# Graph attention and four residual layers on one core: own places for every job of the attention loop, and a reordered last phase

## The chip, the cores and the metric

The kernel runs on one core of one Trainium2 chip. Five engines work side by side, each with its own instruction queue worked off in order: PE (TensorE, matmuls and transposes), DVE (VectorE), ACT (ScalarE), POOL (GpSimd) and SP (SyncE, here only DMA issues). An instruction that needs another engine's result waits on a semaphore, and everything behind it in its queue waits too. The metric is the device time of one execution in microseconds (us); less is better.

## The reference

Sixteen graphs (B = 16) of N = 1024 nodes with F = 128 features and a weighted, symmetric-pattern adjacency of about 9 neighbours a node go through four layers, each `x = layernorm(x + layer(x))`:

```python
# layer 0: graph attention
pre = (h_self @ A1_i)[:, :, None, :] + (h_nb @ A1_j)[:, None, :, :] + A1_b
scores = where(adjacency == 0, -1e9, (relu(pre) @ A2_w)[..., 0] + A2_b[0])
out = relu(h_self + einsum('bij,bjf->bif', softmax(scores), h_nb))
# layer 1: a row-by-row dilation of the pattern, three SAGE convolutions with batch norm, then
out = concatenate([h1, h2, h3], -1) @ Wl + bl
# layer 2
out = relu(adj @ (x @ W + b) + x)
# layer 3
A1 = A + eye(N);  d = rsqrt(sum(A1, -1))
out = ((A1 * d[:, :, None] * d[:, None, :]) @ x) @ B
```

## The kernel before, in words

Four phases follow one another: attention (`phase_att`), the dilation pattern, the convolutions, and End (`phase_end`, which does the sum over the three convolutions, layer 2 and layer 3).

**Attention.** A graph's 1024 nodes are cut into ten groups of 104 (the last has 88). A *block* is one row band of group pairs, `band(r)`: 11 *units*, each a pair (i, j) of groups. Five blocks (r = 0 to 4) make a batch of 55 units; 16 batches make 80 blocks. The neighbours inside a unit are put into up to 128 slots. For each unit PE gathers the projected rows of both ends by one-hot matrices (`gather`, L506, lines 516 and 521), DVE scores both directions (`score`, L533), ACT takes the exponential and weighs the rows (`weigh`, L543 and L545), and three units later PE scatters them into the PSUM sums (`scatter`, L554) with a one-hot matrix that DVE makes (`numbered`, L501). A unit with i = j has one direction ("one way"), the others two.

The one-hot matrices of a block come from a chain of *jobs* that run one to three blocks ahead: counts and offsets of the slots; `beyond` (L369, POOL: the step table g, 1 where the slot number plus one exceeds the unit's offset, else 0, in pieces of 4, 4 and 3 units); `ranks` (L380, PE); `steps` (L409, PE, from g), `others` (L424, PE), `one_way` (DVE), `widen` (ACT), `numbers`. Each batch also makes the ten *projections* of the next one (`projection`, L297: two matmuls into a bank, then six readers of the bank: high, other_z and own on ACT, low, add_z and the self score on DVE, lines 315 to 321), its mask rows (L280 and L282 on POOL, with a load before and a store behind on SP), and the end of the one before: collects of the sums (`collect`, DVE, L565), clears of the sums (`clear`, PE, L264), ten `end_group` on DVE (L598 to L601 and statistics), `end_root` on POOL, ten `end_norm` on ACT (L619), stores, and three `end_turn` (transposes into a bank, read by ACT at L639).

All of these jobs that need PE products put them into a pool of two PSUM banks (`ps_w`, name pw). A new job takes the bank that comes free, and its first matmul waits until the last reader of the previous content is done. The main loop runs over units; for unit u of a block it issues in order: what is due (`later`), the block's jobs for that u, the gather, the products of the job, `numbered`, the score, *all* readers of the job one after the other, the weighing, a scatter. u = 0 to 2 holds the three steps, 3 to 5 the others, 6 and 7 a projection each, 8 to 10 ranks with counts, offsets and numbers. `as_traced` (L131) fixes each engine's order to that of the program from `first` on, in attention only.

**End.** For each batch b: eight tiles of `layer2` (`neighbours` is eight matmuls into one PSUM tile, L1647; DVE L1661 to L1664 and statistics; after tiles 3 and 7 `root`, whose power is on POOL at L1587, and d at L1668 or L1673; after tile 5 `apply` of half 0, DVE L1591), `turn` of both halves (PE transposes L1619, read by ACT L1620), `values_3`, eight tiles of `layer3`. Woven in is the first step of batch b+1: `bias_1` (POOL, L1575), `products_1` (PE, L1603) and `rows_1` (DVE: the sum at L1608, then four tiles' statistics and the root), `apply`, `turn`, `values_2`. `store_slots` (L1519) writes rows kept from the pattern phase into the x rows of batch b+4: two indirect DMAs on POOL, issued in layer 2's tile 5. Their order on the engines is left to the scheduler here.

Of the kernel before, what the change touches and what calls it, by code (L numbers as in the profile page):

```python
# [23 lines left out]
P = 128  # L24
# [86 lines left out]
def constants(arrays):  # L111
# [13 lines left out]
    arrays["k_next"] = np.ascontiguousarray(np.broadcast_to(i + 1, (P, P)).astype(np.float16))  # L125
# [5 lines left out]
def as_traced(tc, first):  # L131

    last = {}
    for i in tc.nc.cur_bb.bb.instructions[first:]:
        if i.engine in last:
            tc.add_manual_dep(
                i, last[i.engine].name,
                mybir.DependencyInfo(mybir.DependencyClass.NoSync, mybir.DependencyReason.DATA),
                reason="as_traced",
            )  # L140
        last[i.engine] = i


@with_exitstack
def phase_att(ctx, tc, t, c, x1_d, x1T_d, mask_d, flags):
# [27 lines left out]
    k_next = load("k_next", [P, C])  # L173
# [123 lines left out]
    def projection(b, s):  # L297

        d = S[b]

        def products():
            pw = d.pw = ps_w.tile([P, 512], F32, name="pw")
# [8 lines left out]
        def readers():  # L311
            pw = d.pw
            hi = d.parts[s] = lp.tile([P, 2, 3 * F], F32R, name=f"parts{s}", bufs=1 if s < 4 else 2)
            z = sm.tile([P, F], F32, name="z_self", bufs=2)
            nc.scalar.copy(hi[:W, 0, :], pw[:W, : 3 * F])
            nc.scalar.copy(z[:W], pw[:W, 2 * F : 3 * F])
            nc.scalar.copy(d.own[:W, s, :, :F], pw[:W].rearrange("p (a f) -> p a f", f=F)[:, ::3, :])  # L317
            nc.vector.tensor_tensor(hi[:W, 1, :], pw[:W, : 3 * F], hi[:W, 0, :], ALU.subtract)  # L318
            nc.vector.tensor_tensor(z[:W], pw[:W, F : 2 * F], z[:W], ALU.add)
            k = b * NG + s  # L320
            nc.vector.scalar_tensor_tensor(
                z[:W], z[:W], 0.0, w_a2[:W], op0=ALU.max, op1=ALU.mult, accum_out=seen_self[:W, k : k + 1]
            )

        return products, readers
# [43 lines left out]
    def beyond(v, n0, m):  # L369

        if n0 == 0:
            v.g = sm.tile([P, UNITS, C], F16, name="g", bufs=1)
        g = v.g[:E, n0 : n0 + m, :]
        nc.gpsimd.tensor_tensor(  # L374
            g, k_next[:E].unsqueeze(1).to_broadcast([E, m, C]),
            v.off[:, n0 : n0 + m].unsqueeze(2).to_broadcast([E, m, C]), ALU.subtract,
        )
        nc.gpsimd.tensor_scalar(g, g, 1.0, 0.0, op0=ALU.min, op1=ALU.max)  # L378
# [77 lines left out]
    def bank_job(*parts):  # L456

        bank = []

        def products():  # L460
            bank.append(ps_w.tile([P, 512], F32, name="pw"))
            for f, g, args, at in parts:
                f(*args, bank[0][:, at:])

        def readers():
            for f, g, args, at in parts:
                g(*args, bank[0][:, at:])

        return products, readers

    def block_job(x, s):

        if s < 6:
            v = block(x + 1)
            f, g = ((steps, copy_steps), (others, copy_others))[s // 3]
            return [bank_job((f, g, (v, *pieces()[s % 3]), 0))] if v else []
        v, w, z = block(x + 2), block(x + 3), block(x + 1)
        parts = []
        if v:
            parts.append((ranks, copy_ranks, (v, *pieces()[s - 8]), 0))  # L480
        if s == 8 and w:
            parts.append((counts, copy_counts, (w,), 4 * W))
        if s == 10 and w:
            parts.append((offsets, copy_offsets, (w,), 4 * W))
        if s == 10 and z:
            parts.append((numbers, copy_numbers, (z,), 4 * W + 16))
        return [bank_job(*parts)] if parts else []
# [170 lines left out]
    def run(*parts):  # L658
        for f in bank_job(*parts):
            f()  # L660

    for x in range(3):
        v = block(x)
        run((counts, copy_counts, (v,), 0))
        run((offsets, copy_offsets, (v,), 0))
        if x == 2:
            break
        for n0, m in pieces():
            beyond(v, n0, m)
        for n0, m in pieces():  # L670
            run((ranks, copy_ranks, (v, n0, m), 0))
        if x == 1:
            continue
        for f, g in ((steps, copy_steps), (others, copy_others)):
            for n0, m in pieces():
                run((f, g, (v, n0, m), 0))
                if f is others:
                    widen(v, n0, m)
        run((numbers, copy_numbers, (v,), 0))
        for half in range(2):  # L680
            one_way(v, half)
    first = len(nc.cur_bb.bb.instructions)
    ORDER = (*range(4, NG), *range(4))
    SLOTS = BANDS * UNITS
    END_GROUP = (6, 7, 10, 11, 16, 17, 21, 22, 27, 28)
    owed, later = [], {}
    ld = {}

    def do(at, f, *args):
        later.setdefault(at, []).append((f, args))  # L690

    def mask_step(b, s):
        store = mask_rows(b, s, ld.pop((b, s)))
        do(at + 3, store)

    for b in range(1, B):
        base = (b - 2) * SLOTS + 40
        for s in range(NG):
            when = base + 4 * s if b > 1 else 3 * s
            do(max(when - 3, 0), lambda b, s: ld.update({(b, s): load_mask_rows(b, s)}), b, s)  # L700
            do(when, mask_step, b, s)
    for at in range(B * SLOTS):
        b, n = divmod(at, SLOTS)
        r, u = divmod(n, UNITS)
        x = at // UNITS
        for f, args in later.pop(at, []):
            f(*args)
        jobs = []
        if u in (6, 7):
            if b + 1 < B:  # L710
                jobs.append(projection(b + 1, ORDER[2 * r + u - 6]))
        else:
            jobs += block_job(x, u)
        v = block(x + 1)
        if v and u in (2, 4):
            one_way(v, u == 4)
        if v and 3 <= u < 6:
            do(at + 1, widen, v, *pieces()[u - 3])
        v = block(x + 2)
        if v and u in (4, 6, 8):  # L720
            beyond(v, *pieces()[u // 2 - 2])
        if b + 1 < B:
            if n == 5:
                begin(b + 1)
            if n == 53:
                do(at + 1, self_weight, b + 1)
        if b:
            if n == 0:
                end_load(b - 1)
            if 3 <= n < 6:  # L730
                collect(b - 1, n - 3)
            if n == 4:
                end_seen(b - 1)
            if n == 6:
                end_divide(b - 1)
                nc.gpsimd.memset(OWN[(b - 1) % 2][:W, :, 0, F : F + 1], 1.0)
            if n in END_GROUP:
                end_group(b - 1, ORDER[END_GROUP.index(n)])
            if n == 30:
                end_root(b - 1)  # L740
            if 33 <= n < 33 + NG:
                end_norm(b - 1, n - 33)
            if n == 45:
                end_store(b - 1)
            if n in (46, 48, 50):
# [1712 lines left out]
```

## Time and profile before

| | us |
|---|---|
| three runs | 3035.19, 3040.84, 3047.08 (median 3040.84) |
| the profiled execution | 3058.9 |
| its span, from first to last instruction | 3056.8 |
| mean granted PE clock | 0.937 |
| attention, about 62 to 1520 | 1458 |
| pattern, about 1520 to 2000 | 480 |
| convolutions, about 2000 to 2335 | 335 |
| End, about 2335 to 3056 | 721 |

The page begins with each engine's busy time and share of the span, and the span in 40 slices, where a digit is the busy share in tenths:

```profile
PE 2723.7 (89%) x25724; PEld 2392.3 (78%) x25724; DVE 2191.9 (72%) x8416; ACT 1860.8 (61%) x5689; POOL 1426.8 (47%) x1545
...
PE   5999999999999999999968888578796999999997
...
DVE  5788888888888888888863567756664666666664
ACT  3888888888888888888862233255654233343332
POOL 3766665666666666666313331244333333233321
PEclk8999999999999999999987777789997999999999
```

A row of a group of instructions has: line, engine, operation, output and input tiles with their shapes, count, then total busy time and mean ns of one, then the engine's idle time ahead of them and who ended it. The groups that the change touches on POOL and DVE:

```profile
L280 POOL TENSOR_SCALAR mask<-ld 104x1024 f16<-104x1024 f32 (+1 forms) x150 | 426.5, 2843 | 39.6 <-DMA ld<-in_adjT 39.4
L374 POOL TENSOR_TENSOR g<-k_next,off 105x512 f16<-105x512 f16 (+1 forms) x240 | 236.4, 985 | 366.4 <-PE pw L411 360.9
L378 POOL TENSOR_SCALAR g<-g 105x512 f16<-105x512 f16 (+1 forms) x240 | 188.7, 786 | 20.7
L318 DVE TENSOR_TENSOR parts<-pw,parts 104x384 fp32r<-104x384 f32 x160 | 88.9, 556 | 123.2 <-ACT own L317 122.0
L1591 DVE TENSOR_SCALAR x<-x,mv,rstd 128x128 f32<-128x128 f32 x256 | 104.7, 450 | 91.2 <-POOL rstd L1587 91.2
```

A row of waits has the engine and line that waited, the instruction it waited for, then total us, how often, and the longest. A timeline row has start, duration, engine, line, operation, tiles and count, and in brackets the idle time ahead of it and what ended it. Instructions of one line in a row are put together (x4). On PE a record's end is modelled and records overlap, so the spacing of starts is the better measure of cost there.

### The profile page before, as it was taken

Reading aid. Unit: us, or ns where it says so; the run is one execution under the profiler, and the core shown is the slowest. Engines: PE = TensorE matmul, PEld = TensorE weight load, DVE = VectorE, ACT = ScalarE, POOL = GpSimd, SP = SyncE. Lnnn points to the kernel's source line nnn. Section 1 sums busy time; section 2 is a strip of 40 time slices with the busy share of each in tenths; the row PEclk is TensorE's granted clock in tenths of the full one; section 3 lists DMA queues with packets and bytes.
Section 4 is the critical chain, followed back from the end, with each engine's and each line's share of the span. In section 5 each row is a group of like instructions: output and inputs, shape, how many; then the busy total and the mean of one; then the engine's idle time right before and its main releaser. Section 6 shows DMA issues by size and latency. Waiting matters only on the chain.

```text
span 3056.8 us, 70983 instructions
## 1 busy us (share of the span) xinstructions
PE 2723.7 (89%) x25724; PEld 2392.3 (78%) x25724; DVE 2191.9 (72%) x8416; ACT 1860.8 (61%) x5689; POOL 1426.8 (47%) x1545
## 2 busy tenths in 40 slices
PE   5999999999999999999968888578796999999997
PEld 3877777777777777777768887377786999999997
DVE  5788888888888888888863567756664666666664
ACT  3888888888888888888862233255654233343332
POOL 3766665666666666666313331244333333233321
PEclk8999999999999999999987777789997999999999
DMA  5323332233322333223026442054455354445440
GB/s 145 100 73 96 102 95 81 71 99 98 93 79 75 103 98 93 76 73 97 22 58 210 145 150 60 17 178 160 169 193 192 113 181 161 147 146 181 160 152 16
DMA packets 179958, 348.60 MB, mean 114 GB/s; under 512 B 14148, under 2 KB 89942, under 8 KB 179472
## 3 DMA queue, kind: packets, MB, share of 16 engines
q1 hardware_dynamic: 173584, 328.15, 33.7%
q0 software_dynamic: 4864, 11.63, 1.3%
q10 hardware_dynamic: 1152, 4.19, 0.5%
q8 instruction: 206, 3.38, 0.5%
q14 instruction: 152, 1.25, 0.1%
HBM read 257.87 MB, written 87.03 MB: 113 GB/s over the span
## 4 chain that ended last, share of the span: by engine, by line
PE 46%; DVE 28%; ACT 9%; issue 7%; DMA 6%; POOL 3%; SPq 0%; POOLq 0%; ACTq 0%; DVEq 0%
PE pg L1647 10%; PE pa L554 5%; DVE junk L533 5%; PE pg L516 4%; PE pg L521 3%; PE pq L1357 3%; DVE we L501 2%; DMA x_d<-keep_xs,keep_row 2%; ACT hg L545 2%; DVE oh_b L435 2%; DVE one_way L403 2%; PE pg L1007 2%; ACT oh L441 2%; DVE st L78 2%; DVE x_rows L601 2%
## 5 line engine op out<-in xcount | busy, mean ns | idle before, releaser
L545 ACT ACTIVATE hg<-pg,hg 128x128 f32<-128x128 f32 x1600 | 510.2, 365 | 28.6
L554 PE MATMUL pa<-hg,we 128*104 128x129 f32 (+1 forms) x3520 | 526.1, 272 | 0.0
L516 PE MATMUL pg<-parts,oh 104*128 104x384 f32 (+1 forms) x1760 | 512.8, 373 | 3.5 <-ACT hg L545 3.3
L554 PEld LDWEIGHTS pa<-hg,we 128*104 128x104 f32 x3520 | 447.7, 171 | 46.5 <-issue 38.2
L533 DVE SCALAR_TENSOR_TENSOR junk<-pg,w_a 128x128 bf16<-128x128 f32 x1600 | 396.7, 281 | 110.9 <-PE pg L521 104.4
L280 POOL TENSOR_SCALAR mask<-ld 104x1024 f16<-104x1024 f32 (+1 forms) x150 | 426.5, 2843 | 39.6 <-DMA ld<-in_adjT 39.4
L521 PE MATMUL pg<-parts,oh 104*128 104x384 f32 (+1 forms) x1760 | 434.3, 328 | 0.0
L374 POOL TENSOR_TENSOR g<-k_next,off 105x512 f16<-105x512 f16 (+1 forms) x240 | 236.4, 985 | 366.4 <-PE pw L411 360.9
L521 PEld LDWEIGHTS pg<-parts,oh 104*128 104x128 f32 x1760 | 311.4, 189 | 0.0
L543 ACT ACTIVATE hg<-sc 128x2 f32<-128x2 f32 (+1 forms) x880 | 187.8, 213 | 160.8 <-DVE junk L533 147.4
L516 PEld LDWEIGHTS pg<-parts,oh 104*128 104x128 f32 x1760 | 268.8, 191 | 21.5 <-ACT oh L441 15.1
L501 DVE TENSOR_TENSOR we<-k_id,ids 128x832 f32<-128x832 f16 (+1 forms) x240 | 259.2, 1080 | 9.3 <-PE pa L554 8.7
L1587 POOL TENSOR_TENSOR rstd<-ve,mhalf 128x4 f32<-128x4 f32 x96 | 97.0, 1011 | 323.9 <-DVE ve L1586 323.8
L441 ACT CAST oh<-oh_b 104x1024 fp32r<-104x1024 bf16 (+1 forms) x240 | 233.4, 973 | 1.0 <-DVE oh_b L435 1.0
L378 POOL TENSOR_SCALAR g<-g 105x512 f16<-105x512 f16 (+1 forms) x240 | 188.7, 786 | 20.7
L303 PE MATMUL pw<-w_all,xT 128*104 128x512 f32 x320 | 172.1, 620 | 24.7 <-ACT x1T L639 9.4
L318 DVE TENSOR_TENSOR parts<-pw,parts 104x384 fp32r<-104x384 f32 x160 | 88.9, 556 | 123.2 <-ACT own L317 122.0
L1591 DVE TENSOR_SCALAR x<-x,mv,rstd 128x128 f32<-128x128 f32 x256 | 104.7, 450 | 91.2 <-POOL rstd L1587 91.2
L435 DVE TENSOR_TENSOR oh_b<-pw,k_slot_edge 104x512 bf16<-104x512 f32 (+1 forms) x240 | 152.6, 636 | 5.6 <-PE pw L427 5.6
L1696 ACT ACTIVATE y<-x,shift,rstd 128x128 f32<-128x128 f32 x128 | 52.7, 482 | 162.9 <-POOL shift L1689 162.9
L403 DVE SCALAR_TENSOR_TENSOR one_way<-qs,mask 104x1040 bf16<-104x1040 f16 (+9 forms) x160 | 146.7, 917 | 1.1 <-ACT qs L396 1.1
L420 ACT CAST oh_b<-pw 104x512 bf16<-104x512 f32 (+1 forms) x240 | 131.2, 547 | 20.4 <-PE pw L411 20.0
(349 smaller groups left out, 6522.1 us busy)
## 6 DMA issues: line engine op xcount, KB each, us to landing
ld<-in_adjT SPq DMA_DIRECT2D x135, 416.0 KB
m<-mask_d SPq DMA_DIRECT2D x16, 2048.0 KB
keep_adj<-in_adjT SPq DMA_DIRECT2D x8, 4096.0 KB
adj<-in_adjT SPq DMA_DIRECT2D x8, 4096.0 KB
mask_d<-mask SPq DMA_DIRECT2D x144, 208.0 KB
hT_d<-uT SPq DMA_DIRECT2D x48, 512.0 KB
h<-hT_d SPq DMA_DIRECT2D x48, 512.0 KB
hT<-hT_d SPq DMA_DIRECT2D x32, 512.0 KB
```

Of the source, the lines that this page charges most:

```text
L280: engine.tensor_scalar(mt[:n, s, :N], ld[:n], 0.0, None, op0=ALU.is_gt)
L374: nc.gpsimd.tensor_tensor(g, k_next[:E].unsqueeze(1).to_broadcast([E, m, C]), v.off[:, n0 : n0 + m].unsqueeze(2).to_broadcast([E, m, C]), ...
L403: nc.vector.scalar_tensor_tensor(junk[:W, :nb, :], v.q[:W, at : at + nb, :W], EDGE, v.mt[:W, i, i * W : NP].rearrange("p (n w) -> p n w", ...
L435: nc.vector.tensor_tensor(v.o[:W, n0 : n0 + m, 1, :], pw[:W, : m * C].rearrange("p (n c) -> p n c", c=C), k_slot_edge[:W].unsqueeze(1).to_ ...
L441: nc.scalar.copy(v.ends[:W, n0 : n0 + m], v.o[:W, n0 : n0 + m])
L501: nc.vector.tensor_tensor(we[:, :n, :], k_id.unsqueeze(1).to_broadcast([P, n, W]), V[b * BANDS + r].ids[:, 2 * lo : 2 * hi].unsqueeze(2).t ...
L516: nc.tensor.matmul(flat[:, first : 3 * F], own, d.parts[i][:W, p, first:], start=p == 0, stop=False, skip_group_check=True,)
L521: nc.tensor.matmul(pg[:, 1::step, :], other, reversed_parts(d.parts[j][:W, p, :], step), start=False, stop=p == 1, skip_group_check=True,)
L533: nc.vector.scalar_tensor_tensor(junk, pg[:, 1 + e, :], 0.0, w_a2, op0=ALU.max, op1=ALU.mult, accum_out=d.sc[:, at + e : at + e + 1],)
L545: nc.scalar.activation(hg[:, e, :F], pg[:, 3 - 3 * e, :], AF.Copy, scale=hg[:, e, F : F + 1])
L554: nc.tensor.matmul(PA[bank][:W, at : at + part.stop - part.start], we[:, 2 * (u - lo) + e, :], hg[:, e, part], start=False, stop=True, ski ...
L1647: nc.tensor.matmul(pg[:, :cols], ADJ[b % 2][:, jt, it * P : (it + 1) * P], v[:, jt, :cols], start=jt == 0, stop=jt == T - 1,)
```

## The change

In attention every job's products and every single reader get a key: a place in units from the start of the block, with a fraction that orders it among the gather (.2), score (.49), weighing (.7) and scatter (.8) of that unit. All entries of all blocks are sorted by their key and issued in that order. A key may lie in the next block (over 11) or the one before (below 0). AHEAD says for which block the job is done. Jobs of the prologue are now the same entries, from block -3 on. The six readers of a projection are taken in the order high, other_z, own, low, add_z, self, at the keys of PROJECT behind the first, in ascending order of the keys.

```diff
+BANKS = (
+    (-1.1, (("step", 0),)), (0.38, (("step", 1),)), (0.72, (("step", 2),)), (1.82, (("other", 0),)),
+    (2.82, (("other", 1),)), (4.52, (("rank", 1),)), (5.3, (("rank", 0), ("count", 0),)), (5.42, (("other", 2),)),
+    (6.38, (("rank", 2), ("number", 0), ("offset", 0),)),
+)
+READ = {
+    ("step", 0): -0.9, ("step", 1): 0.48, ("step", 2): 1.65, ("rank", 0): 5.54, ("count", 0): 5.52, ("other", 0): 1.9,
+    ("other", 1): 3.95, ("other", 2): 5.75, ("rank", 1): 4.58, ("rank", 2): 8.31, ("offset", 0): 6.75,
+    ("number", 0): 8.95,
+}
+PROJECT = (
+    (6.3, 6.95, 6.42, 7.15, 7.25, 6.72, 10.58), (9.85, 10.02, 10.38, 11.1, 10.52, 11.32, 15.02),
+)
+BEYOND = (3.42, 3.48, 6.32)
+NUMBERED = (0.51, 6.9, 9.3)
+ONE_WAY = (-1.48, 0.52)
+WIDEN = (2.25, 6.33, 7.25)
+SCORE, WEIGH, SCATTER = 0.49, 0.7, 0.8
+COLLECT = (2.9, 5.56, 4.54)
+CLEAR = (4.72, 6.3, 5.78)
+DIVIDE = 6.45
+END_GROUP = (6.53, 9.52, 14.34, 8.02, 21.05, 28.95, 24.48, 26.53, 16.25, 28.34)
+END_ROOT = 30.1
+END_NORM = (37.34, 39.56, 36.15, 33.54, 41.3, 33.65, 33.82, 43.52, 44.56, 40.6)
+END_STORE = 45.1
+TURN = ((47.1, 47.48), (48.34, 48.51), (51.56, 52.56))
+MASKS = (-92.64, -89.49, -72.95, -66.46, -62.48, -54.95, -50.1, -47.1, -43.44, -37.5)
+AHEAD = {"step": 1, "other": 1, "number": 1, "rank": 2, "count": 3, "offset": 3}
...
+    for x in range(-3, B * BANDS):
+        b, r = divmod(x, BANDS)
+        at = x * UNITS
+        for u in range(UNITS if x >= 0 else 0):
+            do(at + u, 0.2, open_gather, b, r, u)
+            do(at + u, SCORE, take, score, b, r, u)
+            do(at + u, WEIGH, take, weigh, b, r, u)
+            do(at + u, SCATTER, scatters, b, r * UNITS + u)
...
+    for key, _, f, args in sorted(todo, key=lambda t: t[:2]):
...
+        f(*args)
     as_traced(tc, first)
```

The step table becomes one comparison for each unit, against a table now held in f32:

```diff
-        nc.gpsimd.tensor_tensor(
-            g, k_next[:E].unsqueeze(1).to_broadcast([E, m, C]),
-            v.off[:, n0 : n0 + m].unsqueeze(2).to_broadcast([E, m, C]), ALU.subtract,
-        )
-        nc.gpsimd.tensor_scalar(g, g, 1.0, 0.0, op0=ALU.min, op1=ALU.max)
+        for n in range(n0, n0 + m):
+            nc.gpsimd.tensor_scalar(v.g[:E, n, :], k_next[:E], v.off[:, n : n + 1], None, op0=ALU.is_gt)
```

In End `rows_1` is split into `add_1` (the sum) and `stats_1` (statistics and root), `apply(b, 0)` comes behind bias_1, `store_slots` issues one of its two DMAs behind layer 3's tile 3 and the other behind tile 5, the matmul loops of `turn` and `neighbours` run backwards, and `as_traced` holds the order of the whole phase:

```diff
             if more and it == 4:
                 bias_1(b + 1)
-            if it == 5 and b + 4 < B:
-                with tc.issue_after(S[b].first.ins):
-                    store_slots(nc, x1_d, keep, b + 4)
+            if it == 5:
+                apply(S[b], 0)
         turn(b, 0)
         if more:
             products_1(b + 1, 0, range(4))
-            rows_1(b + 1, 0)
-        values_3(b, 0)
+            add_1(b + 1, 0)
         apply(S[b], 1)
         if more:
             products_1(b + 1, 1, range(2))
         turn(b, 1)
+        for half in range(2):
+            values_3(b, half)
         if more:
             products_1(b + 1, 1, range(2, 4))
-        values_3(b, 1)
+            stats_1(b + 1, 0)
+            add_1(b + 1, 1)
         for it in range(T):
             layer3(b, it)
             if more:
                 if it == 0:
-                    rows_1(b + 1, 1)
                     apply(S[b + 1], 0)
+                if it == 1:
+                    stats_1(b + 1, 1)
                 if it == 2:
-                    apply(S[b + 1], 1)
                     turn(b + 1, 0)
                 if it == 3:
-                    turn(b + 1, 1)
+                    apply(S[b + 1], 1)
...
                 if it == 5:
-                    values_2(b + 1, 1)
+                    turn(b + 1, 1)
                     store(b, 0)
+                if it == 6:
+                    values_2(b + 1, 1)
                 negative(b + 1, it)
+            if it in (3, 5) and b + 4 < B:
+                store_slots(nc, x1_d, keep, b + 4, (it - 3) // 2)
```

## The prediction

> **What bounds the kernel now.** I read the windows by stage first, then what TensorE (PE) waits for in each, then the order of events round these waits. By stage:
>
> ```profile
> core 0: us, PE busy (x) PEld busy (x) DVE busy (x) ACT busy (x) POOL busy (x), PEclk, DMA share, GB/s
> 62.00:1520.00 1458.00, 1390.01 (x12050) 1151.26 (x12049) 1212.03 (x5229) 1225.57 (x3927) 923.36 (x874) 1.00 0.31 86
> 1520.00:2000.00 480.00, 362.54 (x5742) 325.11 (x5741) 293.40 (x962) 158.16 (x431) 142.19 (x218) 0.75 0.34 108
> 2000.00:2335.00 335.00, 277.99 (x2154) 250.70 (x2154) 210.74 (x304) 196.94 (x712) 134.89 (x190) 0.92 0.49 174
> 2335.00:3056.00 721.00, 665.74 (x5634) 651.45 (x5634) 446.46 (x1829) 261.38 (x572) 207.89 (x234) 0.95 0.41 143
> ```
>
> The rows are attention, dilation pattern, convolution layers and End. The change rewrites the first and the last. In attention PE is busy 1390 of 1458 us at full clock, DVE 83%, ACT 84%: PE's matmuls are the same after the change, so waits can give 68 us there at most, and two engines with little slack can take it back. In the stretch 100 to 1500 us this is all that PE waits for:
>
> ```profile
> PE pw L383 <- DVE z_self L319: 33.9, 43, 1.0
> PE pa L264 <- DVE own L565: 12.6, 14, 1.3
> PE pw L303 <- ACT x1T L639: 9.4, 14, 0.7
> PE pw L427 <- DVE oh_b L435: 3.8, 13, 0.3
> PE pw L303 <- DVE oh_b L435: 3.3, 14, 0.2
> ```
>
> 63 us over 13 to 14 batches: ranks waiting for a projection's reader, the clear for a collect, and bank reuse. Over steady batches (period 95.9 us) I count 4.63 us of PE idle each, 15 such batches. One instance, PE then DVE:
>
> ```profile
> 779.94 0.40 PE L521 MATMUL pg<-parts,oh 104*128 104x256 f32 x2
> 781.06 0.34 PE L383 MATMUL pw<-cnt,k_offs 104*128 104x416 f16 x1 [0.72 <-DVE z_self L319]
> ```
>
> ```profile
> 779.39 0.29 DVE L533 SCALAR_TENSOR_TENSOR junk<-pg,w_a 128x128 bf16<-128x128 f32 x1
> 780.16 0.56 DVE L318 TENSOR_TENSOR parts<-pw,parts 104x384 fp32r<-104x384 f32 x1 [0.48 <-ACT own L317]
> 780.64 0.28 DVE L319 TENSOR_TENSOR z_self<-pw,z_self 104x128 f32<-104x128 f32 x1
> ```
>
> The bank may be overwritten only after L319 at 780.92; PE starts .14 us later. That is what a bank wait looks like: last reader's end plus .15.
>
> In End PE's one large wait is the second turn (L1619): 22.3 us in 11 waits between 2400 and 2900. POOL shows why, then PE and DVE:
>
> ```profile
> 2587.93 1.14 POOL L1521 DMA_INDIRECT x_d<-keep_xs,keep_row  x1 [0.19 <-issue]
> 2594.11 0.97 POOL L1521 DMA_INDIRECT x_d<-keep_xs,keep_row  x1 [5.04 <-DMA x_d<-keep_xs,keep_row]
> 2595.09 1.05 POOL L1673 TENSOR_TENSOR d<-deg,mhalf 128x4 f32<-128x4 f32 x1
> 2596.11 1.00 POOL L1587 TENSOR_TENSOR rstd<-ve,mhalf 128x4 f32<-128x4 f32 x1
> 2597.09 2.33 POOL L1575 TENSOR_TENSOR x<-x,keep_bl 128x1024 f32<-128x1024 f32 x1
> ```
>
> ```profile
> 2596.21 1.50 PE L1603 MATMUL pp<-keep_wl,h 128*128 128x128 f32 x12
> 2599.57 1.10 PE L1619 MATMUL pt<-ident,x 128*128 128x128 f32 x4 [1.86 <-DVE x L1591]
> 2600.51 2.72 PE L1603 MATMUL pp<-keep_wl,h 128*128 128x128 f32 x12
> ```
>
> ```profile
> 2597.15 3.14 DVE L1591 TENSOR_SCALAR x<-x,mv,rstd 128x128 f32<-128x128 f32 x4 [3.38 <-POOL rstd L1587]
> ```
>
> The second store waits in POOL's queue for the first; the statistics' power L1587 waits behind it; apply L1591 waits for that; PE stands still 1.86 us. After it the same twelve products take 2.72 us instead of 1.50 and the turn 1.10 instead of .60.
>
> **The change in End.** Turn to turn, batches 1 to 11 take 43.76 us on average, batches 12 to 14 (no store_slots) 40.26. Removing the store from this place is worth the difference, 3.50 us, and its parts agree: idle 2.03 (22.3/11) plus 1.72 of slow matmuls in 9 of the 11 = 3.43. 11 x 3.50 = 38.5 us. The two stores go behind layer 3's tiles 3 and 5. POOL then stands up to 6 us there, and behind it are only root and shift of tile 7, wanted by a store that comes in the next layer 2: nothing, unless the second pair is later than that half.
>
> Added: add_1 of the next batch now stands in DVE's queue ahead of apply(b,1), which turn(b,1) needs. From the end of layer 2 (T): turn .44 + products half 0 2.67 = 3.11; +.2 until DVE starts; add_1 .67 (L1608); four applies at .28 (1.11 for four with POOL idle); +.15: turn(b,1) can start at T+5.2. PE, with values_3(b,0) moved behind the turn, is there at T+3.11+1.33 = 4.44. A wait of .65 to .75, and .15 to .2 at layer 3's start, where ACT still scales v: .85 us in 14 batches = 11.9. End: -38.5 + 11.9 = **-27**. Ends: -38 if the wait is hidden; if each wait is followed by half-speed matmuls, +1.72 more in 14 batches: -3. I take no slowdown, since attention's idles of .7 to 1.07 us show none behind them. The Trainium skill, "TensorE: Matmul & The Clock Gate", Part 1, lets the clock fall only after an idle window of some 3.4 us; the 1.86 us here were enough, so the row decides; by the rule the slow matmuls have another cause and might stay, which would make End -27 + 9 x 1.72 = -11.5.
>
> The reversed turn and neighbours loops let PE wait once, for the last value: the same sum. Earlier h loads (SP) cost no engine.
>
> **The change in attention.** Same matmuls, same DVE and ACT operations; only their places differ, and POOL's beyond, which is two passes of 512 or 384 elements (mean 985 and 786 ns in the page's groups; 3 pieces, 5.3 us a block) and becomes 11 comparisons of 128. Bounds for one: .3 us (slope of L378 between its shapes) and .52 (L280's 2.5 ns an element plus .2): 3.3 to 5.7 us a block. POOL is busy 63% here and the tables are read several units later: nothing, either way.
>
> Now the waits. Most of those listed go: each clear stands .7 to 1.8 units behind its collect, and the ranks no longer meet a fresh projection's bank. Mask rows (L280, 2.84 us of POOL each) come earlier, and their loads and stores with them in SP's queue, ahead of which nothing is late. But new waits come. The two banks are handed out as they come free, and the third step product (key .72) takes the bank of the second projection (9.85). So it waits for add_z (key 11.32, in front of score 0). From the end of unit 10's gather, DVE: .2 latency, two scores .42, self .22, low .47, add_z .28, .15 to PE = 1.74 us. PE meanwhile has scatter .36, a one-way gather .55, step product 1 .23 = 1.14. A wait of **.6 us in every block**, 3.0 a batch: this is L383's wait at another line. In the fifth block the second turn (key 48.34) takes a bank of the first projection: .8. So 3.8 a batch where DVE and ACT otherwise keep up. They don't everywhere: the first block holds three end groups (1.25 us of DVE each) and a collect, and walking DVE there gives 2.45 us of waits, the fourth has six of the norms, 1.63 with ACT nearly full, the others .78, .94, 1.5: 7.3 a batch. The same walk made on the kernel before falls short of its row by some .3 a block, so it isn't generous. Behind these step products wait the next gather and, through it, score and weigh of the new block. I take the middle, 5.5, against 4.63: 15 x .87 = **+13**. Ends: 3.0 (-24) and 7.3 (+40).
>
> A new prologue does the same work interleaved: 0, within 3 us. Pattern and convolution keep their order: 0.
>
> Sum on the profiled execution: 3056.8 - 27 + 13 = 3042.8 span. It ran 3058.9, 0.6% over the median 3040.84; the same -14 from the median gives **3027**.
>
> **A rule that speaks against it.** apply L1591 x4 takes 1.11 us with POOL idle and 3.14 beside bias_1 (L1575). In the new order bias_1 follows layer 2's tile 3 on POOL and may meet apply(b,0) behind tile 5, ahead of turn(b,0). The Trainium skill, "SBUF — State Buffer", section "SBUF: two separate sides", says why: the port pair that DVE and GpSimd share is held for a whole instruction and the other blocks, as the 3.14 shows. By rule and row the price is the one in rival D.
>
> **Rivals.**
> A, the above: own range 3005 to 3045.
> B, the waits in attention shrink to the .6 of each block because DVE's and ACT's loaded spots lie where PE has work: 15 x (3.0 - 4.63) = -24, with End -27: 2990. For it: DVE idles 110 us before its scores, waiting for PE. Against: the walk on the old kernel gave too little.
> C, slower: DVE and ACT fall behind in the first, fourth and fifth blocks, so that projections' banks come free late: +40, prologue +3, End -27: 3041 + 16 = 3057. It decides from 6.4 us of waits a batch, where attention eats End's gain (4.63 + 27/15). For it: 83% and 84% busy, and the longer chain in front of the third step product.
> D, the store's wait is replaced in End: bias_1 holds apply(b,0) up by 2.03 us (3.14 - 1.11). DVE is through tile 5 some 1 us plus the four applies before turn(b,0), so PE waits about 1.05 us, 14 times = 15, and 24 more if matmuls run slow behind it: End -12 to +12, with +13: 3042 to 3066, I say 3050. Against: bias_1 should end before tile 5 does, as it starts when d's power ends and tiles are 1.81 us apart.
>
> **How the numbers follow.** A .38, B .22, C .30, D .10. The measurement can tell about 0.5%, 15.2 us, from no change: bounds 3025.6 and 3056.0. Faster: half of A, all of B = .41. Within: .17 of A, .06 of D, .08 of C = .31. Slower: .22 of C, .04 of D, .02 of A = .28. Range: 2985 (B with End at -32) to 3064 (C with its waits a little longer).
>
> **What would show it.** Right: no PE wait at the ranks' line for z_self, but .5 to .9 us at the step line on add_z in most blocks; End's turn(b,1) idle .5 to .9 instead of 2; End's period 41 us; POOL's store pair behind layer 3. Wrong: End's twelve products still at 2.7 us, or PE idle over 1 us at turn(b,0) (D); a batch of attention over 97.3 us, with PE waiting for ACT or DVE at gathers (C); under 94.5 (B).

## The result and the profile after

The changed kernel takes 3044.06 us (median of 12 runs, 3038.93 to 3049.38), the kernel before beside it 3045.47 (3035.19 to 3049.52): ratio 1.000, 95% interval 0.9988 to 1.0011. No change, where 3027 was forecast.

One caution comes first. The trace of before that the prediction was read from ran 3058.9 us, 13 more than before's median in these runs, and is none of them. The experiments below were measured in four groups, with before's medians at 3060.15, 3061.52, 3059.89 and 3048.53 us: the same kernel runs at two levels, half a per cent apart. That the chip makes the difference isn't shown, since the groups at 3059.89 and 3048.53 both have chip number 8 on the record. Traces from different levels can't be subtracted, so phases are compared here between before_again and after_again, from two groups of the upper level (before at 3060 and at 3062).

By stage, the changed kernel (after, from the group of 3045 us), with the columns of the windows shown before:

```profile
core 0: us, PE busy (x) PEld busy (x) DVE busy (x) ACT busy (x) POOL busy (x), PEclk, DMA share, GB/s
62.00:1520.00 1458.00, 1362.22 (x11918) 1199.59 (x11917) 1155.08 (x5145) 1208.05 (x3883) 1117.31 (x1240) 0.98 0.31 86
2335.00:3042.00 707.00, 655.62 (x5681) 644.77 (x5679) 473.94 (x1836) 265.78 (x576) 213.12 (x240) 0.97 0.42 151
```

In attention PE is busy 28 us less in the same stretch than before (1390), POOL 194 us more (923), and PE's clock isn't full any more (0.98 against 1.00). What PE waits for there, in after_again (100 to 1500 us):

```profile
PE pw L449 <- POOL own L773: 45.4, 14, 3.3
PE pw L449 <- ACT hg L568: 19.4, 32, 1.3
PE pw L449 <- DVE z_self L359: 16.2, 25, 1.9
PE pw L658 <- DVE z_self L359: 6.0, 13, 0.5
PE pw L449 <- POOL g L416: 3.1, 2, 2.3
```

The waits of before are gone, as forecast, and the step product (L449) waits instead. The second and third rows are the forecast bank wait, also where a later event on ACT is named (at 644.61 us a product listed under ACT starts .15 after add_z's end). The fourth is a turn (L658) that waits for a bank in the same way. The first isn't a bank wait: 45.4 us, 3.24 in each batch, for POOL. The comparison that POOL now makes stands in the page of after as:

```profile
L416 POOL TENSOR_SCALAR g<-k_next,off 105x128 f16<-105x128 f32 x880 | 610.6, 713 | 84.1 <-PE pw L449 84.1
```

713 ns for one unit, over the 300 to 520 that bounded it, and 7.8 us a block instead of 5.3. But its length is only half of the story. POOL around the third step product that follows the first block of a batch, in after_again:

```profile
641.54 1.23 POOL L314 TENSOR_TENSOR mask<-mask,off_diag 104x104 f16<-104x104 f16 x1
653.80 0.19 POOL L325 MEMSET sc<- 128x110 f32 x1 [11.04 <-DVE seen_score L603]
653.93 0.14 POOL L327 MEMSET off<- 128x55 f32 x1
654.05 5.45 POOL L416 TENSOR_SCALAR g<-k_next,off 105x128 f16<-105x128 f32 x8
659.48 3.09 POOL L312 TENSOR_SCALAR mask<-ld 104x1024 f16<-104x1024 f32 x1
662.65 0.38 POOL L314 TENSOR_TENSOR mask<-mask,off_diag 104x104 f16<-104x104 f16 x1
663.01 2.84 POOL L416 TENSOR_SCALAR g<-k_next,off 105x128 f16<-105x128 f32 x3
```

POOL does nothing for 11 us. Its next instruction, a memset in `begin` (key 2.0), reuses the buffer that `end_seen` still has to read, and `end_seen` now stands at 6.45. Behind the memset wait beyond, a mask row and the rest of beyond, which ends at 665.8. PE in the same place:

```profile
662.27 0.39 PE L449 MATMUL pw<-g,k_step 105*128 105x512 f16 x1
665.90 0.48 PE L449 MATMUL pw<-g,k_step 105*128 105x384 f16 x1 [3.24 <-POOL own L773]
666.17 1.06 PE L577 MATMUL pa<-hg,we 128*104 128x129 f32 x4
666.89 0.99 PE L539 MATMUL pg<-parts,oh 104*128 104x384 f32 x2
```

The product waits for the last comparison (the memset named stands right behind it), and after the wait the scatter takes 1.06 us instead of .60 and the gather's first half .99 instead of .59: half speed again (the granted clock is .51 and .50 from 665.2 to 672.0).

End does what was said. PE's one wait in the stretch 2400 to 2900 of after, instead of 22.3 us in 11 waits:

```profile
PE pt L1639 <- DVE x L1606: 12.3, 24, 0.5
```

Its period is 41.0 to 41.1 us in every batch (forecast 41.1; in before_again 42.0 to 44.7 where a store stands in the way). It has two waits of about .5: the forecast one at the second turn, and one at the first. The first comes from here (after, POOL, DVE, then PE):

```profile
2379.64 2.36 POOL L1590 TENSOR_TENSOR x<-x,keep_bl 128x1024 f32<-128x1024 f32 x1
```

```profile
2380.14 2.00 DVE L1684 SCALAR_TENSOR_TENSOR x<-o,x 128x128 f32<-128x128 f32 x1
2382.61 1.08 DVE L1606 TENSOR_SCALAR x<-x,mv,rstd 128x128 f32<-128x128 f32 x4
```

```profile
2383.74 0.66 PE L1639 MATMUL pt<-ident,x 128*128 128x128 f32 x4 [0.39 <-DVE x L1606]
```

bias_1 holds up not apply but the addition ahead of it (2.00 us instead of .29), until bias_1 ends at 2382.00. That is rival D's mechanism at about half of the wait that it priced (.49 against 1.05), and without slow matmuls behind it (granted clock 1.00 from 2400 to 2900).

The phases, from PE's first to last instruction, in us:

| | before_again | after_again | difference | forecast |
|---|---|---|---|---|
| attention | 1593.6 | 1607.0 | +13.4 | +13 |
| pattern | 375.5 | 384.4 | +8.9 | 0 |
| convolutions | 338.2 | 340.6 | +2.4 | 0 |
| End | 697.7 | 674.5 | -23.2 | -27 |
| span | 3058.0 | 3057.9 | -0.1 | -14 |

The rest, -1.6, lies between the phases. Attention by this measure includes the prologue and the whole last batch, so it is longer than the stretch 62 to 1520.

### The profile page after: what moved, and what is told of

Read it like the earlier page. It is cut to its first block, busy times and chain, and to the rows that moved or that the text cites. A ratio compares the mean times of both kernels' runs of the same rounds, so it can differ in the third digit from the quotient of the medians.

```text
span 3042.9 us, 71724 instructions
## 1 busy us (share of the span) xinstructions
PE 2689.7 (88%) x25724; PEld 2440.6 (80%) x25724; DVE 2170.9 (71%) x8416; ACT 1858.1 (61%) x5689; POOL 1642.1 (54%) x1945
## 5 line engine op out<-in xcount | busy, mean ns | idle before, releaser
L416 POOL TENSOR_SCALAR g<-k_next,off 105x128 f16<-105x128 f32 x880 | 610.6, 713 | 84.1 <-PE pw L449 84.1
L539 PE MATMUL pg<-parts,oh 104*128 104x384 f32 (+1 forms) x1760 | 524.4, 379 | 0.0
L577 PEld LDWEIGHTS pa<-hg,we 128*104 128x104 f32 x3520 | 478.2, 174 | 32.1 <-issue 27.2
L544 PE MATMUL pg<-parts,oh 104*128 104x384 f32 (+1 forms) x1760 | 440.6, 332 | 0.0
L544 PEld LDWEIGHTS pg<-parts,oh 104*128 104x128 f32 x1760 | 315.9, 191 | 0.0
L539 PEld LDWEIGHTS pg<-parts,oh 104*128 104x128 f32 x1760 | 278.9, 193 | 3.7
L1640 ACT COPY xT<-pt 128x512 f32<-128x512 f32 x64 | 37.5, 586 | 376.2 <-PE pt L1639 343.6
L524 DVE TENSOR_TENSOR we<-k_id,ids 128x832 f32<-128x832 f16 (+1 forms) x240 | 231.9, 966 | 0.0
L335 PE MATMUL pw<-w_all,xT 128*104 128x512 f32 x320 | 167.8, 606 | 12.6 <-DVE part L257 8.5
L449 PE MATMUL pw<-g,k_step 105*128 105x512 f16 (+1 forms) x240 | 89.6, 376 | 96.3 <-POOL own L773 45.2
L441 DVE SCALAR_TENSOR_TENSOR one_way<-qs,mask 104x1040 bf16<-104x1040 f16 (+9 forms) x160 | 139.3, 871 | 4.0 <-ACT qs L434 4.0
L556 DVE DVE_READ_ACCUMULATOR junk<-pg,w_a 128x1 f32 x1600 | 131.9, 82 | 0.0
```

The lines of the kernel that those rows point to most:

```text
L335: nc.tensor.matmul(pw[:W], d.xT[:, s * W : (s + 1) * W], w_all, start=True, stop=False, skip_group_check=True)
L416: nc.gpsimd.tensor_scalar(v.g[:E, n, :], k_next[:E], v.off[:, n : n + 1], None, op0=ALU.is_gt)
L524: nc.vector.tensor_tensor(we[:, :n, :], k_id.unsqueeze(1).to_broadcast([P, n, W]), V[b * BANDS + r].ids[:, 2 * lo : 2 * hi].unsqueeze(2).t ...
L539: nc.tensor.matmul(flat[:, first : 3 * F], own, d.parts[i][:W, p, first:], start=p == 0, stop=False, skip_group_check=True,)
L544: nc.tensor.matmul(pg[:, 1::step, :], other, reversed_parts(d.parts[j][:W, p, :], step), start=False, stop=p == 1, skip_group_check=True,)
L556: nc.vector.scalar_tensor_tensor(junk, pg[:, 1 + e, :], 0.0, w_a2, op0=ALU.max, op1=ALU.mult, accum_out=d.sc[:, at + e : at + e + 1],)
```

## The experiments

Ratios are to the kernel before, in runs of the same group, with the 95% interval. "Against after" uses after_again's ratio, 0.9997.

**before_again**: the kernel before, unchanged.

> The kernel before, unchanged, for a second profile. The trace of record ran 3058.9 us, its runs 3035 to 3050. Theory 1 (that execution was a slow draw): this one has a span of 3043 +- 6, and the 12 to 15 us are missing in one phase; if in End, its periods are 42 to 43 instead of 43.8. Theory 2 (being profiled lengthens this kernel, by its indirect stores): span 3055 or more again while the timed runs are near 3045. Ratio 1.000 +- 0.002 either way.

Measured 3059.6 us, ratio 1.0001 (0.9992 to 1.0010); span 3058.0, attention's batches 95.9 to 97.2, End's periods 42.0 to 44.7 as in the trace of record. Neither theory: profiling adds nothing, since the timed runs lie at 3060 too, and the span is again at the upper level.

**end_only** and **att_only**: the two halves of the change. In att_only `phase_att` and its constants are after's and the rest is before's, in end_only `store_slots` and `phase_end` are after's.

> Attention of before, End of after. Theory (End's gain is what the two traces show, 17.7 us in the phase and 5.2 ahead of it): -23, ratio 0.9925. Rival (the trace of before overstated the stores' cost; attention costs 14 and the sum moved by 1.4, so End gave only 12): -12, ratio 0.996. In both End's period is 41.1 us with waits of 0.5 at each turn.

> Attention of after, End of before. Theory (by the traces attention is 13.7 us longer): +14, ratio 1.0045. Rival (the longer waits of the first block are partly an effect of one execution): +5 or less, ratio below 1.002. Attention's PE waits: step products for POOL 45 us in 14 batches.

end_only: 3038.96 us, 0.993 (0.9915 to 0.9946), -21: the theory. att_only: 3089.46 us, 1.0095 (1.0077 to 1.0114), +29: the loss is real and larger than forecast. In its trace attention is 24.2 longer than in before_again and the pattern 4.5. Its waits are those of after (6.5 us a batch), yet its batches take 97.7 us where after_again's take 97.0. Over ten batches that is 8 us, and the granted clock explains it: .97 in att_only, .98 in after_again, a difference of about 10 us. The same attention is thus 13 to 24 us longer than before's, by how much of it runs at half clock.

**after_again**: the changed kernel, unchanged.

> The changed kernel, unchanged, beside the others of this call. The runs so far were on two chips (before at 3045 and at 3060 us), and on the second the halves gave +29 (attention) and -21 (End). Theory (the change is worth about nothing on both): ratio to before 1.000 to 1.004. Rival (the halves don't add up, as attention's late projections hide something of End): 0.995 or less.

3060.39 us, 0.9997 (0.9983 to 1.0010). -21 and +29 would give 1.0025, so the halves nearly add up.

**store_back**: both stores where they were, the rest as after.

```diff
             if it == 5:
                 apply(S[b], 0)
+                if b + 4 < B:
+                    store_slots(nc, x1_d, keep, b + 4)
...
-            if it in (3, 5) and b + 4 < B:
-                store_slots(nc, x1_d, keep, b + 4, (it - 3) // 2)
```

> After, with both store_slots back behind layer 2's tile 5. Theory (the store's wait in POOL's queue holds root, apply and turn(b,1)): that turn waits 3 us longer and slow matmuls follow, +40 to +55 over after, ratio to before 1.012 to 1.018, in the 11 batches that store. Rival (the gain of End came from the held order and the split sums): +10 or less, ratio below 1.004.

3090.64 us, 1.0098 (1.0083 to 1.0114): +31 against after, less than the theory's 40 to 55, and End's phase is 702.5 us. The second turn waits 1.8 to 3.3 us again in the storing batches. The store's place is all of End's gain; the other edits cost a little (702.5 against 697.7 of before).

**seen_early**: the memset's wait alone.

```diff
-        do(at, DIVIDE, end_seen, b)
+        do(at, 1.96, end_seen, b)
```

> After, with one key changed: end_seen at 1.96 instead of 6.45, ahead of begin's two memsets (2.0) that reuse the buffers which end_seen reads. Theory (POOL stands 11 us in front of these memsets, beyond behind them comes late, and the third step product of each batch's first block waits 3.2 us): that wait falls to 0.6 or less, 15 x 2.6 to 3.2 = -39 to -48 against after, ratio to before 0.984 to 0.988. Rival (a comparison of 713 ns, 7.8 us a block, makes beyond late by itself): the wait stays above 1.5 us and the gain is below 20, ratio above 0.993.

3039.51 us, 0.9929 (0.9913 to 0.9945): -21 against after, between the two. Its waits, 100 to 1500 us:

```profile
PE pw L449 <- DVE z_self L359: 42.4, 34, 2.0
PE pw L449 <- ACT hg L568: 20.2, 39, 1.6
PE pw L658 <- DVE z_self L359: 6.3, 14, 0.5
PE pw L449 <- POOL g L416: 2.9, 1, 2.9
```

In size this is nearer to the rival, but POOL is gone from the top, with its comparisons as they were, so the rival's reason falls. The last piece of beyond and the product, POOL then PE:

```profile
650.59 1.86 POOL L416 TENSOR_SCALAR g<-k_next,off 105x128 f16<-105x128 f32 x3
```

```profile
658.71 0.32 PE L449 MATMUL pw<-g,k_step 105*128 105x384 f16 x1 [1.93 <-DVE z_self L359]
```

beyond is done 6 us ahead of the product. But under its 3.24 lay another wait: add_z, 1.93 us behind the first block. Taking away the later of two events bares the earlier one.

**two_pass**: after with the old beyond at the new places.

```diff
-        for n in range(n0, n0 + m):
-            nc.gpsimd.tensor_scalar(v.g[:E, n, :], k_next[:E], v.off[:, n : n + 1], None, op0=ALU.is_gt)
+        g = v.g[:E, n0 : n0 + m, :]
+        nc.gpsimd.tensor_tensor(
+            g, k_next[:E].unsqueeze(1).to_broadcast([E, m, C]),
+            v.off[:, n0 : n0 + m].unsqueeze(2).to_broadcast([E, m, C]), ALU.subtract,
+        )
+        nc.gpsimd.tensor_scalar(g, g, 1.0, 0.0, op0=ALU.min, op1=ALU.max)
```

> After, with the old beyond (two passes for each piece against the f16 table) at the new keys. Theory (the comparisons are the dearer form: 0.58 to 0.72 us a unit against 0.44, 5.4 us for eight units against 3.5, so that the third piece misses the step product of the first block by 3.2 us): that wait falls to DVE's 1.9 behind it, and the POOL wait of 2.9 in batch 0 goes: -20 to -30 against after, ratio 0.990 to 0.994. Rival (only begin's wait in POOL's queue matters): the wait of 3.2 stays within 0.5, gain under 8.

3095.01 us, 1.0106 (1.0088 to 1.0123): 33 us *more* than after. The wait for POOL did go (0.3 us left), and prologue and batch 0 together took 157 us instead of 164, so far as expected. But the other batches take about 99.4 us. Ten steady batches (3 to 12) of before_again, after_again, seen_s2 (below) and two_pass, in this order:

```profile
core 0: us, PE busy (x) PEld busy (x) DVE busy (x) ACT busy (x) POOL busy (x), PEclk, DMA share, GB/s
343.10:1304.84 961.74, 915.42 (x7931) 756.99 (x7930) 803.00 (x3461) 810.79 (x2592) 614.65 (x581) 1.00 0.32 89
353.57:1323.10 969.53, 906.14 (x7930) 798.63 (x7930) 776.11 (x3462) 805.51 (x2592) 750.28 (x830) 0.98 0.32 88
344.90:1269.82 924.92, 899.84 (x7933) 779.70 (x7932) 775.19 (x3462) 790.29 (x2592) 744.47 (x830) 1.00 0.33 93
351.21:1347.59 996.38, 919.31 (x7930) 797.45 (x7930) 831.99 (x3461) 799.31 (x2592) 632.23 (x580) 0.98 0.31 86
```

With the same instructions DVE is busy 83.2 us a batch in two_pass and 77.6 in after_again; POOL is busy less. The same end group behind the same memsets, in two_pass (DVE, then POOL), then in after_again, where the eight comparisons from 654.05 (above) run beside it:

```profile
660.56 0.85 DVE L625 SCALAR_TENSOR_TENSOR own<-own,rz 104x128 f32<-104x128 f32 x1
```

```profile
660.22 1.04 POOL L416 TENSOR_TENSOR g<-k_next,off 105x512 f16<-105x512 f16 x1
661.35 0.61 POOL L420 TENSOR_SCALAR g<-g 105x512 f16<-105x512 f16 x1
```

```profile
654.37 0.35 DVE L621 SCALAR_TENSOR_TENSOR own<-own,rz 104x128 f32<-104x128 f32 x1
```

Its median from 600 to 1500 us is .53 us in two_pass and .35 in after_again, and over all shapes one_way takes 1185 ns and 878. Half of the 2.7 us by which a batch is longer shows as idle PE, with add_z (L359) as the largest wait, 54.3 us instead of 16.2; the other half shows as longer busy PE and isn't explained. My theory, which counted only POOL's own time, fell: the comparisons are the dearer form for POOL and the cheaper one for the kernel.

**beyond_alone**: the comparisons in the kernel before, nothing else.

> The kernel before with the comparisons alone (all places and End as before). Two passes at the new places cost 35 us more than the comparisons, DVE's mean instruction was 7% longer there. Theory (POOL's long two-pass instructions hold DVE up, some 4 us a batch, and this shows wherever DVE ends a PE wait): -15 to -45 us, ratio 0.985 to 0.995, numbered falls from 1.08 us mean towards 0.97. Rival (at the old places the waits hang on ACT's own copy, and DVE's loss was hidden): -8 or less, ratio over 0.997.

3053.19 us, 0.9985 (0.9975 to 0.9995): -4.6 by the ratio, the rival. numbered (964 ns instead of 1083) and one_way (826 instead of 921) got faster as the theory said, but at the old places little of it shows. One reason is in its waits: the clear's wait for a collect grew from 12.6 us to 22.1. The rival's own reason, ACT's copy, was not tested.

**s2_only** and **seen_s2**: the third step product later, without and with seen_early.

```diff
-(0.72, (("step", 2),))
+(1.3, (("step", 2),))
```

> After, with only the third step product at 1.30 instead of 0.72; end_seen stays at 6.45. Theory (two separate causes: the bank wait of 0.4 to 1 in every block, and POOL's lateness of 3.2 in the first block, of which the later place covers some 2): the first block's wait falls to about 1.2 on POOL, the others go: -45 to -60 against after, ratio 0.980 to 0.985. Rival (POOL's lateness alone counts, the bank waits are taken over by other waits): -25 to -35, ratio 0.988 or more.

> The kernel with end_seen at 1.96, and besides the third step product at 1.30 instead of 0.72: behind the scatter of unit 0 and the gather of unit 1. Theory (this product waits for add_z of the second projection, 4.5 us a batch in the last trace, and PE has 1.1 us of other work to do first): its waits fall below 1.5 us a batch, -40 to -50 against the kernel with end_seen alone, ratio to before 0.977 to 0.981. Rival (DVE is late anyway, and PE then waits at the next gather, other product or scatter): -10 or less, ratio 0.989 or more.

s2_only: 3025.4 us, 0.988 (0.986 to 0.990), -36 against after, which is the rival's number: the first block's product still waits 2.11 for POOL, and other waits come up (10.9 us of PE at L465 for ACT). seen_s2: 2993.71 us, **0.9773** (0.9757 to 0.9789), -68 against after. The theory, and both causes are needed: -21 and -36 apart, -68 together. Its largest waits:

```profile
PE pw L449 <- DVE z_self L359: 11.0, 14, 0.8
PE pg L539 <- ACT hg L568: 9.2, 26, 0.4
PE pw L658 <- DVE z_self L359: 6.3, 14, 0.5
```

2.5 us a batch instead of 6.2, and periods of 92.3 to 92.7.

**all_four**: seen_s2 with the old beyond, the third turn at 51.9, batch 1's masks every 2.6 units.

> Four edits together: end_seen at 1.96, the third step product at 1.30, the old beyond, the third turn at 51.9 instead of 51.56 (its wait of 0.46 a batch), batch 1's masks every 2.6 units instead of 2 (POOL's overload in batch 0). Theory (each removes its own wait): waits in attention under 1.5 us a batch, about -10 against the former kernel, ratio to before 0.974 to 0.978. Rival (what is left is set by DVE and ACT at 83%): no better than the former.

3038.43 us, 0.9919 (0.990 to 0.9937), 45 more than seen_s2. It rests on the theory that fell with two_pass. The old beyond would explain most of the 45 (it cost 33 there), but the four edits were not separated. Spaced at 2.6, masks came too late for the counts (4.8 us of waits).

**best** and **best_2**: seen_s2, the third turn at 51.9, for the last batch values_3(b,0) ahead of turn(b,1), and an end group taken out of the first block.

```diff
-END_GROUP = (6.53, 9.52, 14.34, 8.02, 21.05, 28.95, 24.48, 26.53, 16.25, 28.34)
+END_GROUP = (6.53, 12.6, 14.34, 8.02, 21.05, 28.95, 24.48, 26.53, 16.25, 28.34)
```

That is best; best_2 has 6.53, 8.02, 14.34, 12.6 as the first four.

> The kernel with end_seen at 1.96 and the third step product at 1.30, and besides: the third turn at 51.9, the second end group at 12.6 instead of 9.52 (DVE in the first block, where the product still waits 0.78), and for the last batch values_3(b,0) ahead of turn(b,1), where the trace of after shows a wait of 3.25 with no other work. Theory: -0.45 x 15, -0.6 x 15, -4: about -18, ratio to before 0.970 to 0.973. Rival (other waits take their place): within 6 of the former, 0.976 or more.

> The kernel with end_seen at 1.96, the third step product at 1.30, the third turn at 51.9 and values_3(b,0) ahead of turn(b,1) for the last batch; of the end groups, the second stands at 8.02 and the fourth at 12.6, so that every group is read before the projection of two batches later writes its rows (in the run best the second one came after it). Theory (three end groups in the first block delay add_z there by one group, 1.25 us, of which 0.78 shows as a wait): as best, periods of 91.5, ratio to before 0.971 to 0.975. Rival (best was fast because it skipped the wait for these rows): 0.977, as without these edits.

In best the second end group reads rows that the projection at key 10.52 has already overwritten, so that group's part of the output is changed; it took 2978.84 us, 0.9732 (0.9718 to 0.9745), and its time stands for itself only. best_2 moves a group whose rows are written a block later: 2964.1 us where before took 3048.53, **0.9718** (0.9698 to 0.9737), the fastest of all, with nothing left out. DVE's end groups were the rest of the first block's wait:

```profile
PE pg L539 <- ACT hg L568: 11.7, 36, 0.4
PE pw L449 <- POOL g L416: 3.6, 2, 3.2
PE pw L449 <- ACT ids L492: 2.6, 14, 0.3
```

Waits are 1.5 us a batch, periods 91.4. Of the three edits that best_2 adds to seen_s2, the one for the last batch of End, forecast at -4, gained nothing: the turn's wait falls from 3.26 to 1.43 us, but two waits of .68 and half clock come with it (granted clock .86 instead of 1.00), and the stretch from the last batch's first turn to the end takes 24.8 us instead of 22.3 in seen_s2.

## Why the prediction was right or wrong

**The sum, and the steps that failed.** -14 was forecast and -0.1 came. By the table 8.9 us of the miss lie in the pattern and 2.4 in the convolutions, both put at 0 without a price ("Pattern and convolution keep their order: 0"), and 3.8 in End; the gaps between phases give 1.6 back. Attention met its +13, but not by the sum's mechanism: there the step that failed is POOL's, "the tables are read several units later: nothing, either way". It costs 3.24 us of PE in each of the measured batches, and other terms hid it.

**End: right in mechanism and close in size.** The store's place is the gain (store_back), the period is the forecast one. -27 became -23.2. From the second period on End gives 27.7, but three things were not in the sum. The first period, 38.8 us in before_again, where its second turn doesn't wait, became 41.0. The stretch ahead of the first turn of layer 2 is 1.0 longer. In the last batch no next batch fills PE: turn(b,1) waits 3.26 us and layer 3 another 1.39, and the stretch from its first turn to the end takes 22.3 us instead of 21.1 (in after, with half clock there, 25.9). In the steady period the wait of .49 at the first turn was missed, and the one behind layer 3's start that I had added did not come.

**"Bounds for one: .3 us and .52": wrong.** .58 where POOL runs eight in 4.64 us (seen_early), .71 in the mean of after. The nearest rows were instructions without a per-partition operand or without f32 input; the range should have reached higher. With the masks of batch 1 every two units this also overloads POOL in batch 0: from the start to the first clear of batch 1 it is 8.4 us longer (163.7 against 155.3; 157.0 in two_pass).

**"The tables are read several units later: nothing, either way": wrong, and the costliest step of the mechanism.** I named what stands behind POOL's work but not what stands in front of it. begin's memsets had stood one unit behind end_seen and were now 4.45 units ahead of it, with beyond in the queue behind. That is 3.24 us behind each first block. Taken away alone it is worth 21 us, since add_z's 1.93 lies under it; with the later product 68.

**The bank wait: right in place, and in size within its spread.** .6 was forecast for each block; in after_again the others have .42, .93, .36 and .77. The first block's DVE load was walked to 2.45; bared by seen_early it is 1.93. The second turn was put at .8 and doesn't wait; the third (key 51.56) waits .45. All waits are 6.2 us a batch against the 5.5 that I took, and steady batches are .84 longer than before's (forecast .87).

**Attention's +13.4 is luck.** POOL's share was not in the sum, and the last three blocks had been walked too high. By DVE's first score of each batch, the prologue is 3.2 us longer, batch 0 is 4.9 longer, the 14 batches behind it 11.7, and the last batch is 6.5 *shorter* (74.6 against 81.1). The sum had 15 equal batches and a prologue of 0, within 3; why the last batch gains was not tested. The steady batches' loss is itself a difference. By the rows of ten batches above, PE is idle 1.7 us a batch more than in before_again and busy .9 less, at a lower clock. So "PE's matmuls are the same", and with it 68 us as the most that waits can give, is not strictly so: in seen_s2 PE is busy 90.0 us a batch at full clock, in before_again 91.5. Why was not tested. In att_only the same code costs 24.

**What I didn't price: a gain.** beyond's new form relieves DVE. At the new places it is worth 33 us (two_pass) and at the old ones 5. The Trainium skill, "SBUF — State Buffer", section "SBUF: two separate sides", has the rule I had applied to bias_1 alone: the one of DVE and GpSimd that starts first holds the port pair they share for its whole instruction, and the other blocks; for DVE this concerns operations with two SBUF inputs or in a two-port mode. The .85 us beside the subtraction agrees with it. Here two long passes on POOL hold DVE up more than several short comparisons (.85 against .35); no run here separates length from the number of inputs.

**"Pattern and convolution keep their order: 0": not so.** The pattern takes 375.5 to 375.9 us in all four traces with before's attention (none of them at the lower level) and 371 to 385 with the new one. Its 371 come in the two groups where before runs 3045 and 3049, its 377 to 385 in the others, so at the upper level the new attention costs the pattern 2 to 10 us. The level counts for as much: the changed kernel itself has 371.5 in after and 384.4 in after_again, most of the 15 us between these two executions. What the pattern takes in before at the lower level no trace shows. In before_again and after_again most of the difference arises in its first 75 us, with a lower granted clock (.64 against .82 in the second stretch of some 10 us) and these waits that nothing in the profile releases:

```profile
PE pu L961 <- issue: 2.0, 2, 1.4
```

```profile
PE pu L976 <- issue: 3.4, 2, 2.1
PE pu L959 <- issue: 3.2, 2, 2.8
```

Why is open; no experiment was made on it.

## What to carry to other kernels

When jobs are moved by hand, list for each engine with a slow queue not only who waits for the moved job but which buffer every instruction in front of it reuses: one memset placed ahead of its buffer's last reader held a whole queue for 11 us. Price an instruction on an engine that shares a port by what it does to the other engine too, and test old and new form at the places where they will stand (33 us or 5 for the same edit here). And take differences of traces only where the kernel before runs at the same level.

## What was not expected of the hardware

The same kernel runs at two levels, 3045 to 3049 us and 3060 to 3062, half a per cent apart and more than most terms of this study; chip number 8 shows both.

Half clock on PE comes here in pieces of 3.4 us or a multiple of it: .50 from 659.7 to 663.1 in seen_early, at a wait of 1.93 us, and .51 and .50 from 665.2 to 672.0 in after_again, at one of 3.24. The length of a gap alone doesn't decide. In before the clock is .50 from 641.3 to 644.7 behind gaps of .30, .87 and .23 us, though I had read that nothing slow follows attention's idles. In End's last batch a wait of 3.25 us comes with half clock in after (.50 from 3002.2 to 3012.4), and one of 3.26 with full clock in after_again (1.00 from 3021 to 3031). The .49 and .54 us gaps of End leave it at 1.00. The Trainium skill, "TensorE: Matmul & The Clock Gate", Part 1, speaks of an idle window of some 3.4 us; shorter gaps of these runs were enough, and one of 3.26 was not.
